# A hand-written order of statements put in another order throughout, the ones written by VectorE, seven warm-up products for six

## The chip, the cores and the metric

The kernel runs on one core of a Trainium2 chip. The metric is the device time of one launch in microseconds (us): the median of 3 runs before was 1338.17 (1337.62 to 1338.43). A core has five engines that each work through a queue of their own, in its order: PE (TensorE, the matrix products, with its weight load PEld), DVE (VectorE), ACT (ScalarE), POOL (GpSimd) and SP (SyncE, which issues most of the transfers here). They are held together by semaphores.

## The reference

A cross-attention in fp32 over 64 batch elements b, with 256 rows of x (512 wide), 256 rows of context (384 wide), and a hidden width of 512:

```
text_p  = einsum('bld,dh->blh', x, W_text) + b_text            # 64 x 256 x 512
audio_p = einsum('bsd,dh->bsh', ctx, W_audio) + b_audio        # 64 x 256 x 512
Q = layer_norm(text_p, g1, beta1)
K = layer_norm(audio_p, g2, beta2)
scores = einsum('blh,bsh->bls', Q, K) / sqrt(512)
alpha  = softmax(scores)
H      = einsum('bls,bsh->blh', alpha, audio_p)
H      = einsum('blh,hk->blk', H, W_out) + b_out
return layer_norm(H + x, g_out, beta_out)
```

## The kernel before

One pass over the 64 batch elements. Everything is placed by hand: the whole body stands under `tc.manual_schedule()`, so each engine gets its instructions in the order in which the statements stand in the file, and the framework adds only the semaphore waits between engines that the tiles need. Each batch element goes through seven stages over several rounds: its x and context are loaded and transposed, q and k are projected and normalised, both go out to DRAM and come back transposed, the scores are made, the softmax, the context z, and the output y with its normalisation. In one round of the steady loop (line 1926, b from 3 to 60, 58 rounds) one element is at the scores (`at`, element b), one at its softmax weights and context (`last`, b-1), one at the end of its context and at the output (`old`, b-2; its output object is `y`), one at the last normalisation (`settled`, b-3), and q and k of element b+2 are projected (`q2`, `k2`), k and q of b+1 turned, x and context of b+3 and b+4 loaded and turned. Ahead of the loop the first rounds are written out statement by statement, and behind it the last ones.

The products are cut so that fewer of them are needed. The scores (`score_part`), the context (`z_part`) and q (`Fork`) use seven half-size products for eight; k and the output use fifteen products of thirds (`Thirds`, 171 wide) in five calls, `one` to `five`. That takes many small sums on the other engines: of halves of q on POOL (`query_step`, L869, tile qsum), of the context on POOL (`c_step`, `e_step`), of z on DVE and POOL (`z_step`, L1084, tile zsum, which reads the PSUM tiles ps_z1 and ps_z2 and the SBUF tile zT), and of results in PSUM on DVE (`dve`, L541).

The steps that the prediction follows, with their lines:

- `y.five()` (L585) is the last group of products of one output; its results stand in ps_m, ps_l, ps_n and ps_u.
- DVE takes them out: `plus_ends` and `plus_middle` (L541, tiles n and u), `plus_n0` (tile d), and `last_11`, `last_10`, `last_01`, `last_00` (L707), which write the finished rows yr with their sums. `last_11` and `last_10` write the same row of yr, and so do `last_01` and `last_00`. Between them stand `add_c22` and `add_c21` (L541, they finish a part of zT from ps_z), `reciprocals` (L956) and `turn_c` (L76, the transposes of the next context).
- ACT writes the rest of zT from PSUM: `copy_top` (L1060, from ps_z1) and `copy_two` (L1114, from ps_z2). Then `copy_n1` (L594), for which DVE's `start_t` waits; the gain and bias of the turned queries, `affine_queries(n)` (L527, tile qT, chunks 0 to 3), and the copy of `after_seven` (L753).
- POOL's `query_step(0)` (L869) makes the first query sum from two chunks, and PE's `score_part(1, 7)` (L884, tile ps_sc) needs it for product 7.
- On SP `load_x_rows` (L97), `store` of q and k (L498), `fetch` of them (L73) and `done.store` (L1369), the finished output, stand in one queue.

At the start `keep_busy(6)` gives PE products of a tile of ones, whose result nobody reads, until the first context is there (L187).

Of the kernel before, what the change touches and what calls it, by code (L numbers as in the profile page):

```python
# [22 lines left out]
def kernel(  # L23
# [87 lines left out]
    nc.gpsimd.memset(ones, 1.0)  # L111
# [1288 lines left out]
    keep_busy(6)  # L1400
# [3 lines left out]
    war = []  # L1404
    pool, tag = (once, 'e')
    war.append(pool.tile([P, HC, P], F32, tag=tag, name=f'war_{0}'))
    arrange(war[0], wa_sb[:, 0, :], HC, nc.gpsimd.tensor_copy)
    mean_wa = means(wa_sb, AC, 'mwa')
    k[0] = Projection('k', 0, c_turn.T, wa_sb, ba_sb, AC, ST, bank[0:2])
    k[0].multiply(0, [0])  # L1410
    k[0].multiply(1, [0])
    k[0].multiply(0, [1])
    x_turn = RowTurn(x_0, DC, 'xT')
    x_turn.tile(0)
    ba_row = ba_sb.rearrange('p (o h) -> p o h', o=1)
    mean_ba = means(ba_row, 1, 'mba')
    k[0].multiply(0, [2])
    x_turn.tile(1)
    pool, tag = (work, 'eT')
    war.append(pool.tile([P, HC, P], F32, tag=tag, name=f'war_{1}'))  # L1420
    arrange(war[1], wa_sb[:, 1, :], HC, nc.gpsimd.tensor_copy)
    pool, tag = (work, 'eT')
    war.append(pool.tile([P, HC, P], F32, tag=tag, name=f'war_{2}'))
    arrange(war[2], wa_sb[:, 2, :], HC, nc.gpsimd.tensor_copy)
    turn_weights(0, 1)
    k[0].multiply(1, [1])
    k[0].multiply(1, [2])
    centre(wa_sb, mean_wa, AC)
    mean_wt = means(wt_sb, DC, 'mwt')
    q[0] = Projection('q', 0, x_turn.T, wt_sb, bt_sb, DC, LT, bank[2:4])  # L1430
    q[0].multiply(0, [0])
    q[0].multiply(0, [1])
    q[0].multiply(1, [0])
    k[0].evict(0)
    wa_t = const.tile([P, 11, WP], F32, tag='wa_thirds', name='wa_thirds')
    third_weights(wa_sb, wa_t, [0])
    k[0].evict(1)
    k[0].scales()
    third_weights(wa_sb, wa_t, [1], nc.vector)
    k[0].normalise([0])  # L1440
    q[0].multiply(1, [1])
    q[0].multiply(0, [2])
    q[0].multiply(0, [3])
    q[0].multiply(1, [2])
    cT[1] = turn_c(1)
    turn_weights(1, 1)
    q[0].multiply(1, [3])
    k[1] = Projection('k', 1, cT.pop(1), wa_sb, ba_sb, AC, ST, bank[4:6])
    k[1].multiply(0, [0])
    bt_row = bt_sb.rearrange('p (o h) -> p o h', o=1)  # L1450
    mean_bt = means(bt_row, 1, 'mbt')
    turn_weights(2, 1)
    centre(wt_sb, mean_wt, DC)
    centre(bt_row, mean_bt, 1)
    wa_blocks = third_weights(wa_sb, wa_t, [3])
    q[0].evict(0)
    k[1].multiply(0, [1])
    k[1].multiply(0, [2])
    bt_step = const.tile([P, H2], F32, tag='bt_step', name='bt_step')
    nc.vector.tensor_tensor(bt_step, bt_sb[:, :H2], bt_sb[:, H2:], ALU.subtract)  # L1460
    k[1].multiply(1, [0])
    q[0].evict(1)
    k[0].normalise([1])
    k[0].store()
    turn_weights(3, 1)
    k[1].multiply(1, [1])
    xT[1] = turn_x(1)
    xs_1 = SumX(xT.pop(1), nc.vector)
    xs_1.add(1)
    wt_blocks = weight_sums(wt_sb, DC // 2, 'wtsum')  # L1470
    load_c(2)
    load_x(2)
    k[1].multiply(1, [2])
    k[0].fetch()
    g1_sb, be1_sb, g2_sb, be2_sb, bac_sb = take_columns()
    fold_multiply(1, 0, 1)
    fold_multiply(1, 1, 2)
    q[0].scales()
    folds.append(p_at.tile([P, H], F32, tag='at', name='ps_fold'))
    fold_multiply(2, 0, 1)  # L1480
    centre(ba_row, mean_ba, 1)
    k[1].evict(0)
    q[0].normalise([0])
    xs_1.add(1)
    k[1].evict(1)
    xs_1.add(1)
    q[0].normalise([1])
    nc.vector.tensor_scalar(g2_sb, g2_sb, scale, None, ALU.mult)
    cT[2] = turn_c(2)
    q[0].store()  # L1490
    fold_multiply(0, 0, 1)
    fold_multiply(0, 1, 2)
    cs[2] = Sides(cT.pop(2), 'csum')
    cs[2].add(1)
    xs[1] = xs_1
    q[1] = Fork(1, xs.pop(1).of, wt_blocks)
    q[1].seven()
    load_c(3)
    cs[2].add(1)
    nc.vector.tensor_scalar(be2_sb, be2_sb, scale, None, ALU.mult)  # L1500
    load_x(3)
    xs_1.add(1)
    cs[2].add(1)
    q[0].fetch()
    Fork.seed()
    q[1].one()
    q[1].after_one()
    fold_multiply(0, 2, 3)
    cs[2].add(1)
    q[1].six()  # L1510
    fold_multiply(2, 1, 2)
    fold_multiply(0, 3, 4)
    q[1].after_seven()
    xT[2] = turn_x(2)
    xs[2] = SumX(xT.pop(2))
    xs[2].add(1)
    part = bias_parts()
    q[1].start_q3()
    k[1].square()
    cs[2].add(1)  # L1520
    fold_evict(0)
    q[1].step_r()
    load_c(4)
    q[1].five()
    at_0 = att[0] = Attention(0)
    at_0.k.turn()
    cs[2].add(1)
    q[1].after_five()
    fold_multiply(1, 2, 3)
    q[1].four()  # L1530
    q[1].two()
    q[1].three()
    k[1].scales()
    third_weights(wa_sb, wa_t, [2], nc.vector)
    k[1].normalise([0])
    k[1].normalise([1])
    k[1].store()
    fold_multiply(1, 3, 4)
    ba_delta = third_bias(ba_sb, 'ba_delta')
    Thirds.seed_with(ba_sb)  # L1540
    load_x(4)
    cs[2].add(1)
    k2_0 = k[2] = Thirds('k', 2, cs.pop(2), wa_blocks, ba_sb, ba_delta)
    k2_0.two()
    q[1].square()
    k2_0.one()
    at_0.affine_keys(0)
    third_weights(wa_sb, wa_t, [4], nc.vector)
    cT[3] = turn_c(3)
    cs[3] = Sides(cT.pop(3), 'csum')  # L1550
    cs[3].add(1)
    q[1].scales()
    k2_0.copy_n1()
    q[1].normalise([0])
    fold_multiply(2, 2, 3)
    Fork.seed()
    xs[2].add(1)
    xs[2].add(1)
    xT[3] = turn_x(3)
    fold_multiply(2, 3, 4)  # L1560
    xs[2].add(1)
    cs[3].add(1)
    k2_0.start_t()
    k2_0.three()
    bias_rest(part, 1, 2)
    q[2] = Fork(2, xs.pop(2).of, wt_blocks)
    q2_0 = q[2]
    q2_0.one()
    at_0.q.turn()
    q[1].normalise([1])  # L1570
    k2_0.copy_t()
    fold_evict(1)
    k2_0.start_l0()
    q[1].store()
    at_0.affine_keys(2)
    at_0.affine_queries(3)
    k2_0.start_l1()
    bias_rest(part, 2, 3)
    cs[3].add(1)
    bias_rest(part, 3, 4)  # L1580
    q2_0.seven()
    fold_evict(2)
    q2_0.after_seven()
    cs[3].add(1)
    q2_0.after_one()
    at_0.affine_keys(1)
    k2_0.four()
    at_0.affine_queries(0)
    q2_0.six()
    k2_0.take_m()  # L1590
    k2_0.start_u()
    cs[3].add(1)
    at_0.affine_queries(1)
    k2_0.five()
    k2_0.copy_u()
    wao_room = const.tile([P, HC * H], F32, tag='wo', name='wao_thirds')
    wao_t = wao_room[:, :11 * WP].rearrange('p (n h) -> p n h', n=11)
    third_weights(wao_sb, wao_t, [1])
    q2_0.start_q3()
    beo_sb = row(beta_out, 'beo')  # L1600
    q2_0.step_r()
    at_0.affine_queries(2)
    k2_0.copy_n()
    q2_0.five()
    q2_0.after_five()
    fold_bias(part)
    cT[4] = turn_c(4)
    k2_0.leave_middle()
    cs[3].add(1)
    at_0.affine_keys(3)  # L1610
    k2_0.leave()
    k2_0.leave_ends()
    xs[3] = SumX(xT.pop(3))
    xs[3].add(1)
    k2_0.middle_d()
    var_0 = small.tile([P, 4], F32, tag='var4', name='var')
    k2_0.square(var_0[:, 2:], [0])
    k2_0.middle_sum()
    xs[3].add(1)
    cs[3].add(1)  # L1620
    k2_0.square(var_0[:, 2:], [1])
    xs[3].add(1)
    q2_0.three()
    q2_0.two()
    k2_1 = k[3] = Thirds('k', 3, cs.pop(3), wa_blocks, ba_sb, ba_delta)
    k2_1.one()
    k2_1.copy_n1()
    xs[3].add(1)
    wao_blocks = third_weights(wao_sb, wao_t, [[0, 3], [4, 2]][0])
    q2_0.square(var_0[:, :2], [0])  # L1630
    q2_0.four()
    k2_0.seed()
    k[1].fetch()
    at_0.score(0, 1)
    at_0.score(1, 2)
    at_0.score(2, 3)
    at_0.score(3, 4)
    at_0.score(4, 5)
    xT[4] = turn_x(4)
    q2_0.square(var_0[:, :2], [1])  # L1640
    at_0.score(5, 6)
    at_0.score(6, 7)
    scales_of(q2_0, k2_0, var_0)
    q2_0.normalise([0])
    q2_0.normalise([1])
    Fork.seed()
    k2_1.start_t()
    k2_1.three()
    at_0.score(7, 8)
    k2_1.two()  # L1650
    k[1].turn([0])
    k2_0.normalise([0])
    cs[4] = Sides(cT.pop(4), 'csum')
    cs[4].add(1)
    k2_0.normalise([1])
    last_1 = att[0]
    last_1.maxima()
    k[1].turn([1])
    q[3] = Fork(3, xs.pop(3).of, wt_blocks)
    q2_1 = q[3]  # L1660
    q2_1.one()
    q2_1.after_one()
    k2_1.copy_t()
    q2_1.seven()
    last_1.exponentials([0])
    q[1].fetch()
    k2_1.start_l1()
    cs[4].add(1)
    q2_1.six()
    last_1.exponentials([1])  # L1670
    k2_1.start_l0()
    last_1.reciprocals()
    k2_1.four()
    q2_1.after_seven()
    q[1].turn()
    k2_1.take_m()
# [249 lines left out]
    for b in range(3, B - 3):  # L1926
# [115 lines left out]
        if done: done.store()  # L2042
# [434 lines left out]
```

## Time and profile before

| | before |
|---|---|
| median of 3 runs | 1338.17 us |
| profiled execution | 1337.96 us |
| its span on the core | 1336.2 us |
| PE busy | 99% |
| DVE busy | 93% |
| ACT busy | 87% |
| POOL busy | 86% |
| share of PE in the chain that ended last | 99% |
| DMA over the span | 240 GB/s |

The span is the time from the first to the last instruction that the profiler saw; the execution is 1.8 us longer. A busy share counts the time in which an engine works, pipelined instructions counted once; a row of a timeline gives the start in us, the duration in us, the engine, the line, the operation and its tiles, and in brackets the idle time ahead of it and what ended it. Starts of neighbouring instructions of one engine can lie closer together than their durations, since they overlap.

### The profile page before, as it was taken

How to read it: one execution, taken by the hardware profiler on the slowest of the kernel's cores; microseconds unless marked ns; L12 is line 12 of the kernel's file. 1: busy time of each engine (PE TensorE's matmuls, PEld its weight loads, DVE VectorE, ACT ScalarE, POOL GpSimd, SP SyncE). 2: the span in 40 equal slices, each digit the busy share in tenths (PEclk: the TensorE clock that was granted, in tenths of full speed). 3: DMA queues.
4: the chain of work that ended last, by engine and by line, in shares of the span. 5: the costliest groups of instructions: out<-in, count | busy, mean ns of one | idle time of the engine just before them, and what ended most of it. 6: DMA issues, size and time to landing. Idle time of an engine off the chain costs nothing.

```text
span 1336.2 us, 29969 instructions
## 1 busy us (share of the span) xinstructions
PE 1329.2 (99%) x8495; PEld 1249.4 (94%) x8495; DVE 1244.4 (93%) x3313; ACT 1163.4 (87%) x3310; POOL 1153.6 (86%) x1855
## 2 busy tenths in 40 slices
PE   9999999999999999999999999999999999999998
PEld 5889999999999999999999999999999999999996
DVE  6669999999999999999999999999999999999968
ACT  4898898898998988888988988989889889889885
POOL 5778898898898988988988988988989889889865
PEclk9999999999999999999999999999999999999999
DMA  9888889989888899888888899889888998888773
GB/s 223 222 243 230 239 252 244 250 244 253 250 246 233 257 250 239 257 246 240 251 245 248 250 244 253 246 232 261 248 234 257 252 240 253 245 243 252 210 233 135
DMA packets 448972, 322.24 MB, mean 241 GB/s; under 512 B 153765, under 2 KB 381349, under 8 KB 448806
## 3 DMA queue, kind: packets, MB, share of 16 engines
q1 hardware_dynamic: 448710, 320.20, 85.8%
q8 instruction: 68, 1.11, 0.4%
q14 instruction: 98, 0.80, 0.2%
q10 hardware_dynamic: 96, 0.13, 0.0%
HBM read 203.57 MB, written 116.65 MB: 240 GB/s over the span
## 4 chain that ended last, share of the span: by engine, by line
PE 99%; ACT 0%; DVE 0%; issue 0%; POOL 0%; ACTq 0%; DVEq 0%; POOLq 0%
PE ps_f L733 29%; PE ps_m L557 16%; PE ps_sc L884 14%; PE ps_n L557 11%; PE ps_u L557 8%; PE ps_z L1033 7%; PE ps_l L557 5%; PE ps_z L1095 5%; PE ps_sc L823 1%; PE ps_f L440 0%; PE ps_m L440 0%; PE ps_n L440 0%; PE ps_l L244 0%; PE ps_u L440 0%; PE ps_fold L244 0%; PE ps_m L244 0%
## 5 line engine op out<-in xcount | busy, mean ns | idle before, releaser
L352 POOL TENSOR_TENSOR csum<-csum,cT 128x256 f32<-128x256 f32 x310 | 195.1, 630 | 5.2
L869 POOL TENSOR_TENSOR qsum<-qT 128x256 f32<-128x256 f32 x118 | 113.0, 958 | 98.7 <-ACT qT L527 92.0
L733 PE MATMUL ps_f<-wtsum,xsum 128*128 128x256 f32 x756 | 194.1, 379 | 0.0
L527 ACT ACTIVATE qT<-qT,columns 128x256 f32<-128x256 f32 x256 | 152.7, 598 | 1.8 <-DVE qT L76 1.8
L733 PEld LDWEIGHTS ps_f<-wtsum,xsum 128*128 128x128 f32 x756 | 131.9, 191 | 11.5 <-issue 0.7
L527 ACT ACTIVATE kT<-kT,columns 128x256 f32<-128x256 f32 x256 | 141.9, 610 | 0.0
L733 PE MATMUL ps_f<-wt,xT 128*128 128x256 f32 x504 | 129.5, 379 | 0.0
L884 PE MATMUL ps_sc<-kT,qT 128*128 128x128 f32 x928 | 122.5, 275 | 0.0
L884 PEld LDWEIGHTS ps_sc<-kT,qT 128*128 128x128 f32 x928 | 114.7, 192 | 0.0
L1357 DVE SCALAR_TENSOR_TENSOR yr<-yr,rstd,beo 128x512 f32<-128x512 f32 x120 | 107.9, 899 | 0.1
L884 PE MATMUL ps_sc<-ksum,qsum 128*128 128x128 f32 x696 | 106.0, 275 | 0.0
L884 PEld LDWEIGHTS ps_sc<-ksum,qsum 128*128 128x128 f32 x696 | 97.8, 191 | 3.4 <-DVE ps_sc L541 0.4
L733 PEld LDWEIGHTS ps_f<-wt,xT 128*128 128x128 f32 x504 | 91.0, 190 | 9.7
L1348 DVE SCALAR_TENSOR_TENSOR yr<-yr,nm,go 128x512 f32<-128x512 f32 x124 | 96.8, 781 | 0.0
L488 ACT ACTIVATE kr<-kr,rstd 128x512 f32<-128x512 f32 x126 | 92.5, 737 | 0.1
L1158 ACT ACTIVATE junk<-yr,nm 128x512 f32<-128x512 f32 x124 | 90.2, 728 | 0.2
L314 POOL TENSOR_TENSOR xsum<-xT 128x256 f32<-128x256 f32 x124 | 90.4, 729 | 0.0
L794 ACT ACTIVATE junk<-ps_f 128x512 f32<-128x512 f32 x126 | 75.3, 598 | 16.8 <-PE ps_f L733 15.4
L541 DVE TENSOR_TENSOR ps_l<-ps_m,t 128x171 f32<-128x171 f32 x248 | 83.6, 337 | 6.2 <-ACT t L605 1.5
L804 ACT ACTIVATE qr<-ps_f,rstd 128x512 f32<-128x512 f32 x126 | 87.9, 700 | 0.1
L520 DVE STREAM_TRANSPOSE kT<-kq 128x512 f32<-128x512 f32 x122 | 85.4, 702 | 1.3 <-DMA kq<-kd 1.2
L1095 PE MATMUL ps_z<-eT,c 128*128 128x256 f32 x296 | 84.4, 380 | 0.0
(302 smaller groups left out, 4657.1 us busy)
## 6 DMA issues: line engine op xcount, KB each, us to landing
kd<-kr SPq DMA_DIRECT2D x64, 512.0 KB, 3.1
kq<-kd SPq DMA_DIRECT2D x256, 128.0 KB, 3.2
qd<-qr SPq DMA_DIRECT2D x64, 512.0 KB, 2.8
qq<-qd SPq DMA_DIRECT2D x256, 128.0 KB, 2.9
xq<-in_x_dram SPq DMA_DIRECT2D x252, 128.0 KB, 3.1
x<-in_x_dram SPq DMA_DIRECT2D x63, 512.0 KB, 5.5
out_dram<-yr SPq DMA_DIRECT2D x62, 512.0 KB, 5.1
cq<-in_ctx_dram SPq DMA_DIRECT2D x252, 96.0 KB, 4.1
```

Source lines behind the costliest of these rows:

```text
L314: self.engine.tensor_tensor(*step)
L352: nc.gpsimd.tensor_tensor(*step)
L488: nc.scalar.mul(row, row, self.r[t])
L527: nc.scalar.activation(self.T[:, k, :], self.T[:, k, :], AF.Identity, bias=bet[:, k : k + 1], scale=gam[:, k : k + 1],)
L557: nc.tensor.matmul(place, lhsT=self.sides.of[n], rhs=self.weights[n], start=(n == 14), stop=True, skip_group_check=True,)
L733: nc.tensor.matmul(place, lhsT=side, rhs=w, start=(n == 7 and c == 0), stop=True, skip_group_check=True,)
L869: nc.gpsimd.tensor_tensor(*self.steps[n])
L884: nc.tensor.matmul(self.place(t, m), lhsT=self.qsides[n][:, c], rhs=self.ksides[n][:, c], start=False, stop=True, skip_group_check=True,)
L1033: nc.tensor.matmul(self.zp[{1: 0, 2: 0, 4: 2}.get(n, 1)], lhsT=self.asides[n], rhs=self.bsides[n], start=(n == 7), stop=True, skip_group_c ...
L1095: nc.tensor.matmul(ps, lhsT=c_rows[self.b][:, s, bass.ts(j, P)], rhs=self.eT[:, s, :], start=start, stop=(s == ST - 1), skip_group_check=True,
L1348: nc.vector.scalar_tensor_tensor(row, row, self.nm[:, t : t + 1], go_sb, ALU.add, ALU.mult)
L1357: nc.vector.scalar_tensor_tensor(self.y[:, t, :], self.y[:, t, :], self.r[t], beo_sb, ALU.mult, ALU.add)
```

## The change

The same statements stand in another order, in the first rounds, in the steady round and at the end. Apart from the order two things differ: the ones are written by VectorE, and `keep_busy` makes seven products of them.

```diff
     ones = once.tile([P, P], F32, tag="u3", name="ones")
-    nc.gpsimd.memset(ones, 1.0)
+    nc.vector.memset(ones, 1.0)
...
-    keep_busy(6)
+    keep_busy(7)
```

The first statements of the steady round, before and now (the lines that say nothing of the steps above are left out):

```diff
     for b in range(3, B - 3):
...
-        old.copy_top()
-        cT[b + 3] = turn_c(b + 3)
-        old.copy_two()
-        q2.seven()
-        at.affine_queries(0)
-        k2.one()
-        k2.copy_n1()
...
-        old.add_c21()
-        old.product_sums()
-        old.z_step(0)
-        at.affine_queries(1)
-        at.query_sums()
-        at.query_step(0)
-        old.z_step(7)
-        q2.after_seven()
-        old.z_step(1)
-        k2.start_t()
...
-        at.score_part(1, 7)
...
+        old.copy_two()
+        k2 = k[b + 2] = Thirds("k", b + 2, cs.pop(b + 2), wa_blocks, ba_sb, ba_delta)
...
+        old.add_c21()
+        last.context_sums()
+        cT[b + 3] = turn_c(b + 3)
+        k2.one()
+        q2 = q[b + 2]
+        q2.seven()
+        old.z_step(0)
+        if done: done.store()
+        at.query_sums()
+        old.copy_top()
+        k2.copy_n1()
+        at.affine_queries(1)
+        at.affine_queries(0)
+        q2.after_seven()
+        k2.start_t()
...
+        at.query_step(0)
...
+        old.z_step(1)
+        at.open_scores()
...
+        at.score_part(1, 7)
```

And its last ones:

```diff
-        y.five()
...
-        at.reciprocals()
-        y.plus_n0()
-        last.add_c22()
-        y.plus_middle(x_old, 0)
-        att[b + 1].affine_keys(3)
-        y.last_10()
...
-        y.last_01(x_old)
-        att[b + 1].key_step(2)
-        y.last_11()
-        at.store_e()
-        k2.fetch()
-        load_x_rows(b - 1)
-        k2.seed()
-        y.last_00()
...
+        k2.normalise([1])
+        load_x_rows(b - 1)
+        k2.normalise([0])
+        k2.store()
...
+        y.five()
+        at.exponentials([0])
+        x_new.add(1)
+        y.plus_ends(x_old)
+        at.exponentials([1])
...
+        y.plus_n0()
+        at.reciprocals()
+        y.last_11()
+        at.divide_e([1])
+        y.last_10()
+        y.plus_middle(x_old, 0)
+        at.divide_e([0])
+        y.last_01(x_old)
+        done = settled
+        at.store_e()
+        y.last_00()
```

What that does to the queues is shown at three places. The first is ACT at the change from one round to the next, from the division of the softmax weights (L960, tile e) to the copy of `after_seven` (L753). L571 and L749 seed PSUM for the next products; qT is the turned query tile. Before:

```order
L960 ACTIVATE e_6608<-e_6608,rden 128x256 [waits Activation_49]
L749 COPY ps_f_90<-ps_f_90 128x256 [waits PE_49]
L571 COPY ps_m<-ba 128x2x171
L1060 COPY zT<-ps_z_6561 128x256 [waits PE_49]
L1114 COPY zT<-ps_z_6671 128x256
L527 ACTIVATE qT_6563<-qT_6563,columns 128x256
L594 COPY n_6691<-ps_n 128x171 [waits DVE_49,PE_49]
L527 ACTIVATE qT_6563<-qT_6563,columns 128x256
L753 COPY s_6705<-ps_f_91 128x256
```

And now, at the same place:

```order
L571 COPY ps_m<-ba 128x2x171 [waits DVE_49]
L749 COPY ps_f_90<-ps_f_90 128x256 [waits PE_49]
L960 ACTIVATE e_6625<-e_6625,rden 128x256 [waits DVE_49]
L960 ACTIVATE e_6625<-e_6625,rden 128x256
L1114 COPY zT<-ps_z_6670 128x256 [waits PE_49]
L1060 COPY zT<-ps_z_6511 128x256 [waits DVE_49,PE_49]
L594 COPY n_6701<-ps_n 128x171 [waits PE_49]
L527 ACTIVATE qT_6567<-qT_6567,columns 128x256 x2
L753 COPY s_6705<-ps_f_91 128x256 [waits PE_49]
```

`copy_top` (L1060) stands behind `copy_two` (L1114) and waits for DVE beside PE; the first of the two query chunks (L527), which stood ahead of `copy_n1` (L594), now stands behind it, next to the second.

The second place is DVE behind `y.five`, from `plus_n0` (d) to the first step of z (L1084); the second row before is `add_c22`, and `plus_ends` stands just ahead of these rows both before and now. Before:

```order
L541 TENSOR_TENSOR d<-ps_n,u 128x171 [waits DVE_49]
L541 TENSOR_TENSOR zT<-ps_z_6561,z_6575 128x128 [waits PE_49]
L541 TENSOR_TENSOR u<-ps_u,x_6386 128x171 [waits DVE_49]
L707 SCALAR_TENSOR_TENSOR yr_6420,totals<-d,ps_n 128x170 [waits DMAHW4_49]
L707 SCALAR_TENSOR_TENSOR yr_6420,totals<-ps_l,x_6386 128x2x171
L707 SCALAR_TENSOR_TENSOR yr_6420,totals<-ps_n,n 128x2x171 [waits DVE_49]
L707 SCALAR_TENSOR_TENSOR yr_6420,totals<-ps_u,u 128x170 [waits DVE_49]
L76 STREAM_TRANSPOSE cT_6683<-cq_6432 128x8x3x32 [waits DMAHW6_49,DMAHW5_49,DMAHW3_49]
L541 TENSOR_TENSOR zT<-ps_z_6561,u_6616 128x128 [waits Activation_49]
L1084 TENSOR_TENSOR zsum<-ps_z_6561,zT 128x256 [waits DVE_49,Activation_49,Pool_49]
```

And now:

```order
L541 TENSOR_TENSOR d<-ps_n,u 128x171 [waits DVE_49]
L956 RECIPROCAL rden<-den 128x2 [waits Activation_49]
L707 SCALAR_TENSOR_TENSOR yr_6399,totals<-ps_n,n 128x2x171 [waits DMAHW3_49]
L707 SCALAR_TENSOR_TENSOR yr_6399,totals<-d,ps_n 128x170 [waits DVE_49]
L541 TENSOR_TENSOR u<-ps_u,x_6333 128x171
L707 SCALAR_TENSOR_TENSOR yr_6399,totals<-ps_l,x_6333 128x2x171
L707 SCALAR_TENSOR_TENSOR yr_6399,totals<-ps_u,u 128x170 [waits DVE_49]
L541 TENSOR_TENSOR zT<-ps_z_6511,u_6617 128x128 [waits PE_49]
L76 STREAM_TRANSPOSE cT_6691<-cq_6490 128x8x3x32 [waits DMAHW6_49,DMAHW7_49,DMAHW5_49,DMAHW4_49]
L1084 TENSOR_TENSOR zsum<-ps_z_6511,zT 128x256 [waits DVE_49,Activation_49,Pool_49]
L541 TENSOR_TENSOR ps_u<-ps_n,n_6701 128x171 [waits Activation_49]
```

The two instructions that write one row (ps_n,n and d,ps_n; ps_l,x and ps_u,u) are now neighbours, each second one with a wait of DVE on itself; `add_c21` (zT from ps_z and u) moved ahead of the transposes, and `start_t` (ps_u from ps_n) ahead of the further steps of z. `add_c21` waited for ACT before and waits for PE now.

The third place is the beginning of DVE's and PE's queues (DVE first, then PE), where a + is a row of now and a - a row of before:

```order
+L111 MEMSET ones 128x128
 L127 MEMSET vectors 128x128
 L179 COPY cTr<-c_107 128x384 x2
 L179 COPY xTr<-x_106 128x512 x2
-L187 MATMUL ps_f_91<-ones 128x128 x6
+L187 MATMUL ps_f_91<-ones 128x128 x7
 L202 MATMUL ps_rows<-ident,cTr 128x128 x6
```

The ones are DVE's first instruction, ahead of the vectors of zeros, and a seventh product stands ahead of the transposes of the first context.

More of the change, by code (lines that the diff above doesn't have):

```diff
@@ L1515 @@
[L1515 removed]
+    nc.vector.tensor_scalar(be2_sb, be2_sb, scale, None, ALU.mult)
+    cs[2].add(1)
+    wa_blocks = third_weights(wa_sb, wa_t, [3])
     xs[2].add(1)
[L1517 to L1520, printed above, removed]
[L1521 to L1532 removed]
```

1500 lines of the change are left out of this document (754 added, 746 removed).

## The prediction

> **What bounds the kernel now.** I read the page first, then the busy times by stretch, the waits, and last the timeline of one steady round, engine by engine. From the page, and from the table of busy times (columns: stretch, its length, then busy time of each engine with its instruction count, granted clock, DMA share, GB/s):
>
> ```profile
> span 1336.2 us, 29969 instructions
> PE 1329.2 (99%) x8495; PEld 1249.4 (94%) x8495; DVE 1244.4 (93%) x3313; ACT 1163.4 (87%) x3310; POOL 1153.6 (86%) x1855
> 0.00:8.00 8.00, 6.43 (x21) 4.67 (x22) 1.27 (x3) 2.86 (x5) 1.98 (x11) 1.00 0.72 212
> 8.00:30.00 22.00, 22.00 (x68) 10.69 (x67) 16.86 (x33) 11.49 (x27) 15.04 (x23) 1.00 0.99 224
> 700.00:720.29 20.29, 20.29 (x136) 19.46 (x135) 19.57 (x54) 18.09 (x53) 18.11 (x30) 1.00 0.87 250
> 1310.00:1337.00 27.00, 21.06 (x93) 15.80 (x91) 20.86 (x50) 13.70 (x36) 13.95 (x17) 0.97 0.26 98
> ```
>
> PE has no idle time in the stretch from 8 to 30 us nor in the round shown, and 1329.2 of 1336.2 in all; a round of the steady loop is 20.29 us of pure matrix work. The change takes no matrix product away, so there is nothing to win in the 58 rounds (the loop runs b from 3 to 60): a new order can only keep PE fed or fail to. What could be won lies in the first 8 us, 8.00 - 6.43 = 1.57, and in the last 27, 27.00 - 21.06 = 5.94, and those are mostly the first load and the last row's normalisation. What could be lost is any wait inside the round, times 58. So the question is one of slack in the round: DVE is busy 19.57 of 20.29, and every chain that leaves PE, crosses other engines and comes back has to fit.
>
> **The start.** The ones now come from DVE.
>
> ```profile
> 1.30 0.20 POOL L111 MEMSET ones<- 128x128 f32 x1
> 1.56 2.93 PE L187 MATMUL ps_f<-ones 128*128 128x128 f32 x12 [1.56 <-POOL ones L111]
> 0.82 0.17 DVE L127 MEMSET vectors<- 128x128 f32 x1 [0.82 <-PEq L2465]
> 3.88 1.20 DVE L179 COPY cTr<-c 128x384 f32<-128x384 f32 x2 [2.90 <-DMA c<-in_ctx_dram]
> 4.49 1.54 PE L202 MATMUL ps_rows<-ident,cTr 128*128 128x128 f32 x6
> ```
>
> DVE's first instruction starts at 0.82, POOL writes the ones at 1.30, so PE can begin 0.48 earlier; the seventh product costs 2.93/6 = 0.49, which takes that up exactly. What follows, the transposes at 4.49, waits for DVE's copy of c at 3.88 and that for a load, which nothing here brings forward. I take 0; the bounds are -0.5 (the whole 0.48 reaches the end) and +0.5 (the seventh product in the way of the transposes). The other statements ahead of the loop and behind it do the same work in another order. Between 8 and 30 us PE had no gap to lose; I take 0, between -1 (some of the last 5.94) and +1.5 (one late input of the size of the 1.57 in the first 8 us).
>
> **The steady round.** One chain changes its form. `y.five` ends with its sums in ps_m, and DVE then runs twelve instructions from `plus_ends` to `add_c21` and `turn_c`, with `z_step(0)` as the thirteenth. Before, ACT's `copy_top` waited for PE alone and had run long before `z_step(0)`; now it waits for DVE too, and the semaphore count that it waits for is the one that `z_step(0)` raises in the built program. Behind `copy_top` in ACT's queue stand `copy_n1`, the affines of query chunks 1 and 0, and `after_seven`. For the affines waits POOL's `query_step(0)`, and for that PE's product 7 of the scores. DVE's side of it, as it ran before (start, duration):
>
> ```profile
> 702.94 0.51 DVE L541 TENSOR_TENSOR n<-ps_m,x 128x342 f32<-128x342 f32 x1
> ...
> 703.99 0.28 DVE L541 TENSOR_TENSOR zT<-ps_z,z 128x128 f32<-128x128 f32 x1
> 704.18 0.33 DVE L541 TENSOR_TENSOR u<-ps_u,x 128x171 f32<-128x171 f32 x1
> 704.42 0.33 DVE L707 SCALAR_TENSOR_TENSOR yr<-d,ps_n 128x170 f32<-128x170 f32 x1
> ...
> 704.67 0.51 DVE L707 SCALAR_TENSOR_TENSOR yr<-ps_l,x 128x342 f32<-128x342 f32 x1
> ...
> 705.79 0.97 DVE L76 STREAM_TRANSPOSE cT<-cq 128x768 f32<-128x768 f32 x1
> 706.69 0.25 DVE L541 TENSOR_TENSOR zT<-ps_z,u 128x128 f32<-128x128 f32 x1
> 707.62 0.41 DVE L1084 TENSOR_TENSOR zsum<-zsum,ps_z 128x256 f32<-128x256 f32 x1
> ```
>
> *DVE.* From 702.94 to 706.69 eleven of the instructions take 3.75; `add_c21` adds 0.19 (704.18 - 703.99, the same operation and size). In the new order `last_11` is followed at once by `last_10`, and `last_01` by `last_00`, each pair writing one row, with a wait of DVE on itself. What such a pair costs stands in the trace ahead of the loop, where they were neighbours already:
>
> ```profile
> 95.32 0.33 DVE L707 SCALAR_TENSOR_TENSOR yr<-d,ps_n 128x170 f32<-128x170 f32 x1
> ...
> 95.68 0.51 DVE L707 SCALAR_TENSOR_TENSOR yr<-ps_n,n 128x342 f32<-128x342 f32 x1
> ...
> 96.12 0.33 DVE L707 SCALAR_TENSOR_TENSOR yr<-ps_u,u 128x170 f32<-128x170 f32 x1
> ...
> 96.50 0.51 DVE L707 SCALAR_TENSOR_TENSOR yr<-ps_l,x 128x342 f32<-128x342 f32 x1
> ```
>
> A 170-wide one is followed after 0.36 and 0.38 here, and after 0.25 in the loop (704.42 to 704.67): 0.11 + 0.13 = 0.24 for the two pairs. `z_step(0)` itself takes 0.41. DVE's part: 3.75 + 0.19 + 0.24 + 0.41 = 4.59 from the start of `plus_ends`.
>
> *ACT and POOL.* Their rows before:
>
> ```profile
> 705.85 0.37 ACT L1060 COPY zT<-ps_z 128x256 f32<-128x256 f32 x1
> 706.12 0.38 ACT L1114 COPY zT<-ps_z 128x256 f32<-128x256 f32 x1
> 707.29 0.30 ACT L594 COPY n<-ps_n 128x171 f32<-128x171 f32 x1 [0.30 <-PE ps_n L557]
> 707.49 0.60 ACT L527 ACTIVATE qT<-qT,columns 128x256 f32<-128x256 f32 x1
> 708.00 0.36 ACT L753 COPY s<-ps_f 128x256 f32<-128x256 f32 x1
> 711.76 0.59 ACT L527 ACTIVATE qT<-qT,columns 128x256 f32<-128x256 f32 x1
> 708.18 0.73 POOL L869 TENSOR_TENSOR qsum<-qT 128x256 f32<-128x256 f32 x1
> 712.43 1.19 POOL L869 TENSOR_TENSOR qsum<-qT 128x256 f32<-128x256 f32 x1 [1.58 <-ACT qT L527]
> ```
>
> `copy_top` holds ACT 0.27 (705.85 to 706.12), `copy_n1` 0.20, the first affine 0.51, the second runs its whole 0.60: 1.58. POOL's step takes 0.73. From engine to engine: ACT to POOL 712.43 - (711.76 + 0.59) = 0.08; POOL to PE 1.56 - (1.30 + 0.20) = 0.06; for DVE to ACT I take 0.05. The chain is 4.59 + 1.58 + 0.73 + 0.19 = 7.09 and ends 702.94 + 7.09 = 710.03 on the clock of this round.
>
> *PE.* Between `y.five` and product 7 stand the same products before and now, in a slightly different order:
>
> ```profile
> 702.74 0.45 PE L557 MATMUL ps_u<-wao_thirds,zT 128*128 128x171 f32 x2
> ...
> 704.55 0.39 PE L1033 MATMUL ps_z<-eT,c 128*128 128x128 f32 x2
> ...
> 709.27 0.50 PE L884 MATMUL ps_sc<-ksum,qsum 128*128 128x128 f32 x3
> 95.22 0.49 PE L1033 MATMUL ps_z<-eT,c 128*128 128x128 f32 x2
> ```
>
> PE would be there at 709.27. Before, `query_step(0)` was done at 708.18 + 0.73 = 708.91, 0.36 ahead of need; now it is 710.03 - 709.27 = 0.76 late. A product that PE had to wait for also starts with nothing loaded behind it: 0.49 after the wait at 95.22 against 0.39 in the stream, 0.10 more. So 0.86 a round, and since the chain starts at PE's own `y.five`, PE's delay moves the next round's chain by as much and nothing makes it up: 58 x 0.86 = 49.9. Bounds: 0.70 a round (engine hops of 0.05, the reload hidden behind another wait's end) gives 40.6; 0.96 (the next products, which need `step_r` from the same ACT queue, pay a second reload) gives 55.7.
>
> [...]
>
> *Transfers.* SP's queue moves too: `load_x_rows` now stands ahead of `k2.store`, so the keys' way out and back starts later by that issue.
>
> ```profile
> 705.75 1.95 SPq L73 DMA_DIRECT2D kq<-kd  x4
> 707.74 0.88 SPq L97 DMA_DIRECT2D x<-in_x_dram  x1
> 712.94 0.70 DVE L520 STREAM_TRANSPOSE kT<-kq 128x512 f32<-128x512 f32 x1
> kq<-kd SPq DMA_DIRECT2D x256, 128.0 KB, 3.2
> ```
>
> The fetch was issued by 705.75 + 1.95 = 707.70 and landed 3.2 later, at 710.9, for a transpose at 712.94: 2.0 of cover against at most 0.88. I take 0; without that cover `turn` and all of DVE behind it would stand 0.88. `done.store` comes earlier in the queue and nobody waits for it in the round.
>
> **Sum.** The profiled execution took 1337.96, span 1336.2 with 1.8 around it; the median of the runs is 1338.17, 0.2 above. 1337.96 + 49.9 + 0 = 1387.9; I say 1388.
>
> **Rivals.** *A: no loss.* DVE is through `z_step(0)` earlier than I add up. If `z_step(0)` is done 0.76 sooner, product 7 is ready when PE comes, PE stays full, and the time is 1337.96 plus or minus the 0.5 of the start, 1337.7 if half of that is won. For it: several waits of DVE for PE and for DMA inside that run are gone or stand elsewhere, and my 0.24 for the pairs and 0.19 for the hops, 0.43 together, may be too much. Against: in the rows above each of DVE's instructions starts before the one ahead has ended, so there was no idle time in the run that could go, and 0.43 is short of 0.76. 8%.
>
> *B: only DVE's own loop is too long.* If the way through PE is covered better than reckoned, DVE still stands between `z_step(0)` and `start_t`: hop 0.05, `copy_top` 0.27, `copy_n1` 0.30, hop 0.08 = 0.70. With the 0.24 of the pairs and its 19.57 of work that is 20.51 against 20.29, 0.22 a round, 12.8 in all: 1351. For it: DVE is the fullest of the four helpers. Against: the way through PE needs 7.09 whatever DVE's sum is. 12%.
>
> *C: POOL's step meets DVE.* `query_step(1)` took 1.19 in this round where `query_step(0)` took 0.73, with DVE's 512-wide instructions running beside it. If the moved step fell beside such a one, 0.46 more a round, 26.7 in all: 1415. [...] Against: behind `z_step(0)` DVE has only short instructions that read PSUM. 8%.
>
> **How the numbers follow.** The forecast has 72%: 1388, alone 1378 to 1396. The range of 8 in 10 reaches down to the upper part of B and up part of the way to C: 1356 to 1400. A measurement of this kernel tells 0.2% (2.7 us) from no change. Faster by over that needs A with a gain at both ends: 4%. Within it, A without: 4%. Slower: all the rest, 92%.
>
> **What would show it.** Right: PE or its weight load waits for POOL's qsum at L869 some 58 times, 0.7 to 0.8 us each; ACT's copy at L1060 waits for DVE's zsum at L1084; a round of 21.1 us, PE busy in some 96% of a steady stretch; DVE, ACT and POOL as busy in total as before. DVE's same-row neighbours at L707 0.11 to 0.13 further apart. The first product near 1.1 us, the transposes of c still near 4.5. Wrong: rounds of 20.3 (A) or 20.5 with PE waiting for DVE and not for qsum (B), or qsum steps of 1.2 in the chain (C). A wait of PE at another product, for a transpose that waits for a load, would say that I followed the wrong chain.

## The result and the profile after

The changed kernel takes 1385.97 us (median of 4 runs, 1384.91 to 1386.67) against 1338.3 before (4 runs): 3.5% slower, ratio 1.0351 with an interval of 1.0333 to 1.0369. The prediction said 1388. The profiled execution took 1385.45, its span 1383.7, so 47.5 more than the span before.

First where the time went. The page of the changed kernel, and the memset of the scores' tile, which runs once a round in both kernels (the view of one line: count, shortest/median/longest in ns, first and last start), of before and then of the change:

```profile
span 1383.7 us, 29786 instructions
PE 1353.1 (98%) x8497; PEld 1250.4 (90%) x8497; DVE 1254.3 (91%) x3314; ACT 1155.3 (83%) x3310; POOL 1167.3 (84%) x1854
```

```profile
L874 DVE MEMSET ps_sc<- x58: 272/272/272, 99.4 to 1256.3; 128x256 f32 x58
```

```profile
L874 DVE MEMSET ps_sc<- x58: 272/272/272, 100.4 to 1304.2; 128x256 f32 x58
```

Between 58 memsets lie 57 rounds: (1256.3 - 99.4) / 57 = 20.30 us before and (1304.2 - 100.4) / 57 = 21.12 now. The 0.82 a round times 58 is 47.7, all of the loss: the start and the end together cost and gain nothing that can be told. PE is counted busy for 1353.1 instead of 1329.2 with one product more. So the busy share hides half of the stall, 23.9 of 47.7: the group of products ahead of the stop is written down as a longer one (ps_u below, 0.53 for 0.45).

The waits of the changed kernel (engine, what waited, for what: total us, times, longest):

```profile
ACT zT L1060 <- DVE zsum L1084: 72.6, 58, 1.4
POOL qsum L869 <- ACT qT L527: 58.4, 58, 1.2
DVE ps_u L541 <- ACT n L594: 45.5, 63, 3.0
PE ps_sc L884 <- DVE ps_sc L874: 22.6, 58, 0.4
```

`copy_top` (L1060) waits for `z_step(0)` (L1084) in each of the 58 rounds, and `start_t` (ps_u, L541) for `copy_n1` behind it. PE, which waited nowhere in the round before, stops 58 times, and the view names the memset of ps_sc, not POOL's qsum. (It also has the weight load of product 1 waiting 35.9 us, 58 times, and names ACT's copy s of L753. That copy cannot be what holds product 1: in a run below, start_t and three later, product 1 starts at 714.13 while the copy runs from 713.80 to 714.16.) The timeline of the round at 711 us, PE first, then DVE, ACT and POOL:

```profile
711.77 0.74 PE L557 MATMUL ps_m<-wa,csum 128*128 128x171 f32 x4
712.45 0.53 PE L557 MATMUL ps_u<-wa_thirds,csum 128*128 128x171 f32 x2
713.37 0.68 PE L884 MATMUL ps_sc<-kT,qT 128*128 128x128 f32 x4 [0.39 <-DVE ps_sc L874]
713.89 0.61 PE L884 MATMUL ps_sc<-ksum,qsum 128*128 128x128 f32 x4
```

```profile
706.76 0.51 DVE L541 TENSOR_TENSOR n<-ps_m,x 128x342 f32<-128x342 f32 x1
...
710.88 0.38 DVE L1084 TENSOR_TENSOR zsum<-ps_z,zT 128x256 f32<-128x256 f32 x1
711.96 0.34 DVE L541 TENSOR_TENSOR ps_u<-ps_n,n 128x171 f32<-128x171 f32 x1 [0.70 <-ACT n L594]
...
712.95 0.27 DVE L874 MEMSET ps_sc<- 128x256 f32 x1
```

```profile
711.35 0.37 ACT L1060 COPY zT<-ps_z 128x256 f32<-128x256 f32 x1 [1.37 <-DVE zsum L1084]
711.62 0.31 ACT L594 COPY n<-ps_n 128x171 f32<-128x171 f32 x1
711.82 1.10 ACT L527 ACTIVATE qT<-qT,columns 128x256 f32<-128x256 f32 x2
```

```profile
713.00 0.73 POOL L869 TENSOR_TENSOR qsum<-qT 128x256 f32<-128x256 f32 x1 [1.00 <-ACT qT L527]
```

The same products of PE in the kernel before (product 7, at 709.27, stands in the prediction):

```profile
707.96 0.74 PE L557 MATMUL ps_m<-wa,csum 128*128 128x171 f32 x4
708.54 0.45 PE L557 MATMUL ps_u<-wa_thirds,csum 128*128 128x171 f32 x2
708.83 0.61 PE L884 MATMUL ps_sc<-kT,qT 128*128 128x128 f32 x4
```

Read from the top: in the round before, ps_u followed ps_m by 0.58 (707.96 to 708.54), product 1 of the scores followed by 0.29 (708.83), and product 7 by 0.44 (709.27). Now the steps are 0.68, 0.92 and 0.52: late by 0.10, 0.63 and 0.08, together 0.81. The first 0.10 belongs to `start_t`: ps_u starts 0.15 behind its end (711.96 + 0.34 = 712.30). Two ways lead from `copy_top` to these products. One is the forecast's: affines, done at 712.92, POOL's qsum, done at 713.73, product 7 at 713.89. The other runs over `copy_n1`, `start_t` at 711.96, two more steps of z and the memset, done at 713.22, to product 1 at 713.37. They end so near each other that this profile cannot say which one costs the time. The experiments were made for that, and for whether `copy_top` is behind both.

### The profile page after: what moved, and what is told of

Same layout as the page of the kernel before. It is cut to its first block, busy times and chain, and to the rows that moved or that the text cites. A ratio compares the mean times of both kernels' runs of the same rounds, so it can differ in the third digit from the quotient of the medians.

```text
span 1383.7 us, 29786 instructions
## 1 busy us (share of the span) xinstructions
PE 1353.1 (98%) x8497; PEld 1250.4 (90%) x8497; DVE 1254.3 (91%) x3314; ACT 1155.3 (83%) x3310; POOL 1167.3 (84%) x1854
## 3 DMA queue, kind: packets, MB, share of 16 engines
q8 instruction: 68, 1.11, 0.4%
## 4 chain that ended last, share of the span: by engine, by line
PE 25%; ACT 24%; DVE 21%; DMA 16%; issue 7%; SPq 6%; DVEq 0%; POOL 0%; ACTq 0%
DMA kd<-kr 8%; PE ps_f L733 6%; SPq L73 6%; PE ps_m L557 4%; ACT kr L488 4%; DVE zsum L1084 4%; ACT kT L527 3%; ACT qr L804 3%; PE ps_sc L884 3%; ACT junk L460 3%; DMA xq<-in_x_dram 3%; DVE yr L1357 2%; ACT junk L794 2%; PE ps_n L557 2%; PE ps_u L557 2%
## 5 line engine op out<-in xcount | busy, mean ns | idle before, releaser
L352 POOL TENSOR_TENSOR csum<-csum,cT 128x256 f32<-128x256 f32 x310 | 250.6, 816 | 0.6
L733 PE MATMUL ps_f<-wtsum,xsum 128*128 128x256 f32 x756 | 184.8, 379 | 0.0
L527 ACT ACTIVATE qT<-qT,columns 128x256 f32<-128x256 f32 x256 | 148.7, 608 | 1.7 <-DVE qT L76 1.7
L884 PE MATMUL ps_sc<-kT,qT 128*128 128x128 f32 x928 | 127.0, 280 | 22.7 <-DVE ps_sc L874 22.6
L733 PEld LDWEIGHTS ps_f<-wtsum,xsum 128*128 128x128 f32 x756 | 136.1, 190 | 14.0 <-issue 0.5
L884 PEld LDWEIGHTS ps_sc<-kT,qT 128*128 128x128 f32 x928 | 112.6, 191 | 36.5 <-ACT s L753 35.9
L527 ACT ACTIVATE kT<-kT,columns 128x256 f32<-128x256 f32 x256 | 142.9, 619 | 1.4 <-DVE kT L520 1.4
L869 POOL TENSOR_TENSOR qsum<-qT 128x256 f32<-128x256 f32 x118 | 86.3, 732 | 59.2 <-ACT qT L527 58.4
L1357 DVE SCALAR_TENSOR_TENSOR yr<-yr,rstd,beo 128x512 f32<-128x512 f32 x120 | 125.4, 1045 | 0.0
L1023 POOL TENSOR_TENSOR esum<-eT 128x256 f32<-128x256 f32 x59 | 43.2, 732 | 89.5 <-DVE eT L76 85.8
L541 DVE TENSOR_TENSOR ps_l<-ps_m,t 128x171 f32<-128x171 f32 x248 | 82.0, 331 | 5.3 <-ACT t L605 3.0
L488 ACT ACTIVATE kr<-kr,rstd 128x512 f32<-128x512 f32 x126 | 85.1, 732 | 0.1
L541 DVE TENSOR_TENSOR ps_u<-ps_n,n 128x171 f32<-128x171 f32 x124 | 42.2, 341 | 45.5 <-ACT n L594 45.5
```

Of the source, the lines that this page charges most:

```text
L352: nc.gpsimd.tensor_tensor(*step)
L488: nc.scalar.mul(row, row, self.r[t])
L527: nc.scalar.activation(self.T[:, k, :], self.T[:, k, :], AF.Identity, bias=bet[:, k : k + 1], scale=gam[:, k : k + 1],)
L541: nc.vector.tensor_tensor(o, i0, i1, op)
L733: nc.tensor.matmul(place, lhsT=side, rhs=w, start=(n == 7 and c == 0), stop=True, skip_group_check=True,)
L884: nc.tensor.matmul(self.place(t, m), lhsT=self.qsides[n][:, c], rhs=self.ksides[n][:, c], start=False, stop=True, skip_group_check=True,)
```

## The experiments

Each is an edit of the changed kernel, but for the third, which edits the kernel before. Times are medians; the ratio is to the runs of the kernel before in the same set, whose median was 1339.95 in the first four, 1340.3 in the next four and 1339.82 in the last two. The round comes from the row of the memset, as above.

| | time, us | ratio and interval | round, us |
|---|---|---|---|
| old round put back | 1340.09 | 1.0002 (0.9993 to 1.0011) | 20.33 |
| copy_top ahead of z_step(0) | 1340.94 | 1.0008 (0.9999 to 1.0017) | 20.33 |
| before, with copy_top behind z_step(0) | 1414.26 | 1.0549 (1.0531 to 1.0568) | 21.60 |
| same-row pairs apart | 1379.93 | 1.0294 (1.0279 to 1.0310) | 21.00 |
| affines first | 1386.54 | 1.0347 (1.0331 to 1.0362) | 21.12 |
| whole queue first | 1357.5 | 1.0131 (1.0116 to 1.0146) | 20.62 |
| start_t and three later | 1385.75 | 1.0339 (1.0314 to 1.0363) | 21.11 |
| both ways shortened | 1368.3 | 1.0208 (1.0188 to 1.0229) | 20.82 |

**The old round put back.** The steady loop of the kernel before, between the new first statements and the new end.

> The changed kernel with the old steady round put back: the new first statements, the new end, VectorE's ones and seven products stay. Theory (all of the loss lies in the 58 rounds): 1338, within 1.5 us of the kernel before. Rival (part of the loss is made at the start and the end, or the round takes over a backlog from the new start): over 1343.

1340.09, no difference to the kernel before that can be told. So the loss is in the loop, and the new start (VectorE's ones, seven products) and the new end are worth nothing either way.

**copy_top ahead of z_step(0).** One statement of the loop is moved:

```diff
         old.add_c21()
+        old.copy_top()
         last.context_sums()
...
         old.z_step(0)
-        old.copy_top()
         k2.copy_n1()
```

> The changed kernel with one statement moved: copy_top stands right behind add_c21, ahead of turn_c and z_step(0), all else as in the change. Theory (copy_top behind z_step(0) holds ACT, and with it start_t, the memset of the scores, the affines and query_step(0)): copy_top starts 1.2 us earlier in the round, by more than the 0.82 that a round lost, so PE waits no more and the time is 1338 to 1342. Rival (the loss is spread over the new order: POOL's longer sums, the same-row pairs on DVE, more transfers at one time): under half comes back, over 1362.

1340.94: of the 46 that lay between the two kernels 45 are back. The stretch of one round, and ACT's row in it:

```profile
700.00:720.33 20.33, 20.33 (x136) 19.50 (x135) 19.94 (x54) 18.08 (x53) 18.32 (x30) 1.00 0.83 240
```

```profile
707.85 0.39 ACT L1114 COPY zT<-ps_z 128x256 f32<-128x256 f32 x1
708.23 0.37 ACT L1060 COPY zT<-ps_z 128x256 f32<-128x256 f32 x1
```

`copy_top` follows `copy_two` after 0.38, where it followed after 1.73 in the changed kernel (709.62 to 711.35), and PE is busy in all of the 20.33. The place of this one statement is the whole loss; 179 others stand where the change put them.

**before, with copy_top behind z_step(0).** The same defect put into the kernel before, with the change's order on ACT:

```diff
-        old.copy_top()
...
-        at.affine_queries(0)
         k2.one()
-        k2.copy_n1()
...
         old.z_step(0)
+        old.copy_top()
+        k2.copy_n1()
         at.affine_queries(1)
+        at.affine_queries(0)
```

> The kernel before with copy_top, copy_n1 and both affines put behind z_step(0), in the change's order on ACT; all else as before. Theory: copy_top starts at z_step(0)'s end + 0.09, then 0.27 + 0.20 + 1.10 on ACT, 0.08, 0.73 on POOL, 0.06 to 0.16: product 7 of the scores comes 0.73 to 0.82 late, 1380 to 1386. Rival (the order on ACT alone does little, and it takes the rest of the new order too): under 1355.

1414.26: the loss is there, and 28 us above the theory's range. PE's first stop is the theory's: product 7 stands 2.06 behind ps_m (704.76 to 706.82) where 1.31 would do (707.96 to 709.27), 0.75 late for the 0.73 to 0.82 that were said. The waits, and PE's second stop, which the theory did not have:

```profile
ACT zT L1060 <- DVE zsum L1084: 82.3, 58, 1.7
ACT ps_m L571 <- DVE kr L541: 32.6, 58, 1.1
DVE zsum L1084 <- ACT zT L1060: 28.9, 58, 0.8
```

```profile
713.23 0.82 PE L557 MATMUL ps_n<-wao,zsum 128*128 128x171 f32 x4 [0.17 <-DVE kr L541]
```

In this order DVE waits for `copy_top` in its turn (28.9 over 58 rounds, 0.50 each) and so comes late to the sums of k (kr). For them waits ACT's next seed of ps_m, 0.56 a round, and PE stops once more, at the first products of y. Those start 1.19 behind the group before them (712.04), which had followed its own by 0.87 (711.17). The mechanism is confirmed. Its price in another order was not to be had by carrying the chain of one round over.

**Same-row pairs apart.**

```diff
         y.last_11()
-        at.divide_e([1])
-        y.last_10()
         y.plus_middle(x_old, 0)
-        at.divide_e([0])
         y.last_01(x_old)
+        y.last_10()
+        at.divide_e([1])
+        at.divide_e([0])
```

> The changed kernel with VectorE's last sums in the order last_11, plus_middle(0), last_01, last_10, last_00, so that no two neighbours write one row. Theory (these two waits of DVE on itself lie on the chain, 0.22 to 0.24 a round): 13 us come back, 1371 to 1375. Rival (they do not lie on the path that sets the end, or the waits only move): 1385 to 1387.

1379.93: 6 of the 13 us come back, which neither had. DVE's four sums in the changed kernel, then its rows here, and PE's last product of z here:

```profile
707.94 0.49 DVE L707 SCALAR_TENSOR_TENSOR yr<-ps_n,n 128x342 f32<-128x342 f32 x1
...
708.47 0.33 DVE L707 SCALAR_TENSOR_TENSOR yr<-d,ps_n 128x170 f32<-128x170 f32 x1
...
708.98 0.50 DVE L707 SCALAR_TENSOR_TENSOR yr<-ps_l,x 128x342 f32<-128x342 f32 x1
...
709.52 0.34 DVE L707 SCALAR_TENSOR_TENSOR yr<-ps_u,u 128x170 f32<-128x170 f32 x1
```

```profile
706.05 0.49 DVE L707 SCALAR_TENSOR_TENSOR yr<-ps_n,n 128x342 f32<-128x342 f32 x1
...
706.47 0.33 DVE L541 TENSOR_TENSOR u<-ps_u,x 128x171 f32<-128x171 f32 x1
706.72 0.51 DVE L707 SCALAR_TENSOR_TENSOR yr<-ps_l,x 128x342 f32<-128x342 f32 x1
...
707.14 0.33 DVE L707 SCALAR_TENSOR_TENSOR yr<-d,ps_n 128x170 f32<-128x170 f32 x1
...
707.40 0.33 DVE L707 SCALAR_TENSOR_TENSOR yr<-ps_u,u 128x170 f32<-128x170 f32 x1
...
707.77 0.29 DVE L541 TENSOR_TENSOR zT<-ps_z,u 128x128 f32<-128x128 f32 x1
```

```profile
707.35 0.39 PE L1033 MATMUL ps_z<-eT,c 128*128 128x128 f32 x2
```

Each 342-wide sum is followed after 0.42 now, where a same-row neighbour followed after 0.53 and 0.54. The pairs did cost 0.23. But `add_c21` needs PE's last product of z, which ends at 707.35 + 0.39 = 707.74, and starts at 707.77, 0.37 behind its neighbour instead of 0.26. From `plus_ends` to `add_c21` the run is 2.91 (704.86 to 707.77) against 3.02 (706.76 to 709.78): 0.11 is left, 58 times of which is 6.4.

**Affines first, and start_t later.** These two take one of the two ways away each. Affines first:

```diff
         old.copy_two()
+        at.affine_queries(1)
+        at.affine_queries(0)
...
         old.copy_top()
         k2.copy_n1()
-        at.affine_queries(1)
-        at.affine_queries(0)
```

> The changed kernel with affine_queries(1) and (0) put right behind copy_two on ACT, into the 1.37 that ACT stands idle ahead of copy_top. Theory (two ways in one: copy_n1, start_t, the steps of z and the memset still wait for copy_top, so product 1 stays where it was): only the 0.08 at product 7 comes back, 1379 to 1384. Rival (the chain of the prediction alone, affines to query_step(0) to product 7): all comes back, 1338 to 1345.

1386.54, nothing came back, not even the 0.08 at product 7. POOL, DVE and PE:

```profile
712.49 0.73 POOL L869 TENSOR_TENSOR qsum<-qT 128x256 f32<-128x256 f32 x1
```

```profile
713.49 0.27 DVE L874 MEMSET ps_sc<- 128x256 f32 x1
```

```profile
713.91 0.68 PE L884 MATMUL ps_sc<-kT,qT 128*128 128x128 f32 x4 [0.39 <-ACT t L605]
714.43 0.61 PE L884 MATMUL ps_sc<-ksum,qsum 128*128 128x128 f32 x4
```

qsum is done at 713.22, long before product 7 at 714.43, and product 7 still follows product 1 by 0.52. So in the changed kernel the 0.08 there was no wait for qsum either, it goes with the stop at product 1. Product 1 starts 0.15 behind the end of the memset (713.76). The bracket names ACT's t (713.56 to 713.86), which product 1 does not read; the memset ends last among what it needs, and product 1 stands 0.15 behind it as in the changed kernel. The way over `start_t` and the memset holds PE by itself for all of the 0.82.

The other way was tried first in a form that is no fair test:

> The changed kernel with start_t behind z_step(1) on VectorE, as it was before the change. In the changed kernel PE stops at product 1 of the scores, released by the memset of ps_sc, and product 7 stands close behind the qsum that it needs. With start_t moved the two steps of z and the memset come 0.46 earlier, so the memset's release of product 1 goes from 713.37 to some 712.99. Theory (two ways in one: product 7's sum on POOL is done at 713.73 whatever the memset does): nothing comes back, 1383 to 1387. Rival (the memset alone sets the stop, product 7 only follows): 0.38 a round come back, 1362 to 1367.

> Both edits at once: start_t behind z_step(1), both affines behind copy_two. Theory (each way alone holds PE, together they are open): the products of k2.two for start_t are now last, 0.35 a round late, 1357 to 1363. Rival (another wait of about the same length stands behind): over 1375.

Both put `start_t` behind `k2.three` too. There it overwrites product 9 of k's projection, which is left out of the result, and it has to wait for that product first: 1404.18 and 1404.13 us, ratio 1.0476 (1.0459 to 1.0494) and 1.0479 (1.0463 to 1.0495), with DVE waiting 28.8 us at `start_t` in the first. (The view names ACT's qT there, which `start_t` does not read; in the round at 722 us product 9 ends at 723.10 and `start_t` starts at 723.21.) They say nothing on the question. With `three` moved along:

```diff
         k2.copy_n1()
...
-        k2.start_t()
...
-        k2.three()
         old.z_step(1)
+        k2.start_t()
+        k2.three()
         at.open_scores()
```

> The changed kernel with start_t behind z_step(1) on VectorE, and k2.three behind start_t, so that product 9 is added to what start_t wrote, as in the changed kernel. The memset of ps_sc comes some 0.46 earlier, product 1 could start at 713.07 on the profiled round's clock (the first affine's end 712.92 + 0.15) where it started at 713.37. Theory (a second way of the same length: the qsum of product 7 is done at 713.73, and a product starts 0.15 after its release, at 713.88 as now): 1383 to 1387. Rival (the way over start_t and the memset is the only one that holds PE, as it holds it alone with the affines moved): 0.3 a round come back, 1366 to 1371.

1385.75, again nothing. The memset, POOL's sum and PE:

```profile
713.62 0.27 DVE L874 MEMSET ps_sc<- 128x256 f32 x1
```

```profile
713.98 0.73 POOL L869 TENSOR_TENSOR qsum<-qT 128x256 f32<-128x256 f32 x1 [1.01 <-ACT qT L527]
```

```profile
713.77 0.53 PE L557 MATMUL ps_u<-wa_thirds,csum 128*128 128x171 f32 x2 [0.27 <-DVE ps_u L541]
714.13 0.61 PE L884 MATMUL ps_sc<-kT,qT 128*128 128x128 f32 x4
714.77 0.71 PE L884 MATMUL ps_sc<-ksum,qsum 128*128 128x128 f32 x4
```

Product 1 now follows ps_u without a wait for the memset, which was done 0.24 before, and product 7 stands 0.64 behind product 1 and 0.06 behind the end of qsum (714.71). Here the forecast's chain is seen with its own stop, and the round is as long as in the changed kernel (21.11 against 21.12). One thing keeps this from being as clean a test as the run before: `start_t` now stands behind `z_step(7)`, which waits 0.49 for `copy_top`, and holds ps_u by 0.43 (712.76 to 713.77, where 0.58 would do), so PE is late by that way too. That qsum alone would cost the whole is read from its row and not from the time: its chain does not run over `start_t`, so product 7 could not start before 714.71 whatever ps_u does.

**Both ways shortened.** Both edits at once.

> The same with both affines right behind copy_two, so that both ways are shorter. Theory: start_t is what is late now, k2.two's last product 0.35 a round, and up to 0.08 for the stopped stream: 1358 to 1366. Rival (a third wait of the old length stands behind the two): over 1375.

1368.3, some 18 back; the theory's range was missed by 2.3. PE's only stop is now at ps_u, for `start_t` (the bracket names POOL's qsum, done at 704.26, which ps_u does not read):

```profile
703.88 0.34 DVE L541 TENSOR_TENSOR ps_u<-ps_n,n 128x171 f32<-128x171 f32 x1
```

```profile
703.35 0.74 PE L557 MATMUL ps_m<-wa,csum 128*128 128x171 f32 x4
704.36 0.53 PE L557 MATMUL ps_u<-wa_thirds,csum 128*128 128x171 f32 x2 [0.27 <-POOL qsum L869]
704.73 0.61 PE L884 MATMUL ps_sc<-kT,qT 128*128 128x128 f32 x4
```

`start_t` ends at 704.22 and ps_u starts 0.14 later, 1.01 behind ps_m where 0.58 would do, and product 1 follows after 0.37 for 0.29: 0.43 + 0.08 = 0.51 a round, where 0.35 was expected for the first part. That there were two ways is shown: neither edit alone gave anything, together they gave 0.30 a round. The 0.51 that is left still comes from `copy_top`: `z_step(7)` waits 0.49 a round for it (28.6 us in all), and `start_t` stands behind that step.

**Whole queue first.** `copy_top` stays behind `z_step(0)`, and what stood behind it goes ahead of it.

```diff
         old.copy_two()
+        at.affine_queries(1)
+        at.affine_queries(0)
...
         old.z_step(0)
...
+        k2.copy_n1()
         old.copy_top()
-        k2.copy_n1()
-        at.affine_queries(1)
-        at.affine_queries(0)
```

> The changed kernel with both affines behind copy_two and copy_n1 ahead of copy_top: copy_top still waits for z_step(0), but only the copy of after_seven stands behind it. Theory (the cost lies in what is queued behind copy_top; of that only z_step(7), z_step(1) and the memset are left, which need copy_top's own result, 0.2 a round): 1349 to 1354. Rival (copy_top's own lateness is the cost, whatever stands behind it): over 1375.

1357.5, some 28 back, 3.5 us above the expected range. DVE and PE:

```profile
718.31 0.34 DVE L541 TENSOR_TENSOR ps_u<-ps_n,n 128x171 f32<-128x171 f32 x1
...
719.44 0.27 DVE L874 MEMSET ps_sc<- 128x256 f32 x1
```

```profile
719.34 0.45 PE L557 MATMUL ps_u<-wa_thirds,csum 128*128 128x171 f32 x2
719.86 0.68 PE L884 MATMUL ps_sc<-kT,qT 128*128 128x128 f32 x4
720.38 0.61 PE L884 MATMUL ps_sc<-ksum,qsum 128*128 128x128 f32 x4
```

`start_t` comes in time. The memset still needs two steps of z that read what `copy_top` wrote or come behind it; it ends at 719.71, product 1 starts 0.15 later and 0.23 late, and product 7 another 0.08 late. So 0.50 of the 0.82 a round was the queue behind `copy_top`, and the rest is its own result that the steps of z wait for.

## Why the prediction was right

**What bounds the kernel, and where a loss could be.** Right: PE still sets the time, the loss is 58 times one stall, and with the old round put back nothing is left of it.

**The start: 0.** Right. VectorE's ones let PE begin at 1.04 where it began at 1.56, the products of ones take 3.35 for 2.93 with the seventh, which takes up 0.42 of that 0.52, and the transposes of c start at 4.66 for 4.49, behind DVE's copy of c at 3.96 for 3.88; nothing of that can be told in the time.

**The chain through DVE, ACT and POOL.** Right in each of its members, to a few hundredths. From `plus_ends` to the end of `z_step(0)` it said 4.59, and it was 711.26 - 706.76 = 4.50; the 0.41 that it took for `z_step(0)` was read from the row of the next step (zsum<-zsum,ps_z is `z_step(1)`), and `z_step(0)` itself took 0.38. `copy_top` 0.27, `copy_n1` 0.20, both affines 1.10 for 1.11, the hop to POOL 0.08 and qsum 0.73 are as said. The hop from DVE to ACT was 0.09 for 0.05. The chain ended 713.73 + 0.06 - 706.76 = 7.03 behind `plus_ends`, with the 0.06 from POOL to PE that the run of start_t and three later shows; 7.09 was said. Product 7 came at 7.13, since product 1 ahead of it was late. The 0.24 for the same-row pairs was 0.23, but only 0.11 of it could be had back, because PE's last product of z stands close behind.

**What PE loses: 0.86 a round.** The size was 0.82; 58 x 0.04 = 2.3 is about the whole distance of 2.0 from 1388 to the result. In the sum stood 0.76 for the chain and 0.10 for a stream that starts with nothing loaded: in the kernel before, the weight load of the product at 95.22 starts at 95.21, after a wait of 0.43, and in the stream that of the product at 704.55 starts at 704.34. In the changed kernel these parts cannot be seen, since product 7 did not wait there. Where it did wait, in the run of start_t and three later, product 7 came 0.70 late (712.76 to 714.77, 2.01 for 1.31), and the group behind it followed after 0.55 (at 715.32) for 0.45: the 0.10 is there.

**Where PE stops.** Here the mechanism had a hole, in one step: "For the affines waits POOL's `query_step(0)`, and for that PE's product 7 of the scores" follows one of two ways only. PE's waits name the memset at product 1, and the sign that was given, 58 waits for qsum, did not show in the changed kernel. It showed as soon as the memset was earlier: with start_t and three later, PE's weight load waits 58 times for qsum, 12.7 us in all. The second way, from `copy_n1` over `start_t` and the steps of z to the memset, had been looked at as far as `start_t`: the idle time of 0.70 reckoned there in rival B is the 0.70 in the row of `start_t`. It was weighed as a matter of DVE's sum and not as a chain that comes back to PE. Both ways are equally long to within 0.1 us, and so the time came out right from the one that does not hold PE in the changed kernel. That is luck: had the second way been half a microsecond longer, 1388 would have been too low by some 29 us. Of the other signs, a share of 96% for PE in a steady stretch came out as 98% (20.73 of 21.12), for half of the stall is counted as busy.

**The rivals.** A (no loss) fell: ACT waits 58 times, 72.6 us in all, for `z_step(0)`. B (only DVE's own loop, 1351) fell: DVE has 1.4 of 21.12 to spare in the round (19.75 busy), and PE is what stops. Half of B's sign did show, since PE waits for DVE and not for qsum, but in rounds of 21.12 and not of 20.5. C (a slow sum on POOL) fell: the view of the line gives qsum a median of 731 ns and a longest of 751, against 738 and 1265 before. What made the long ones before, no run here shows.

Whether `copy_top` must wait for another reader of ps_z1 is not shown: no run left the wait out. What the trace shows is the wait itself: ACT stood 1.25 a round (72.6 / 58) behind a DVE step that writes nothing of what `copy_top` reads. The two steps share ps_z1, which both read, and the tile zT, which `copy_top` writes and `z_step(0)` reads in another part. The waits in DVE's queue speak against zT as the cause: `add_c21` writes zT too, and before, where it followed `copy_top`, a reader of ps_z1, it waited for ACT; now, where it follows only `copy_two`, which writes zT and reads ps_z2, it does not. The order of the two readers is what can be chosen, and that was worth 45 us.

**Transfers.** The earlier `load_x_rows` cost nothing, as said: DVE's waits for the keys (kT for kq) are 2.2 us in three places of the whole span, against 1.2 in one before, and none of them comes back each round.

## What to carry to other kernels

Here ACT's copy from a PSUM tile waited 1.25 us a round for a DVE sum that only reads that tile and stands ahead of it in the program, and with the copy listed first it followed its neighbour after 0.38 without a wait. So try the reader with the longer queue behind it first: one copy behind a sum of 0.38 cost 3.5% here. When a wait in an in-order queue comes late, follow everything that stands behind it in that queue, and everything that waits for that, back to the bound engine; two ways of equal length hid each other here, and a fix of one alone showed nothing (1386.54 and 1385.75 for 1385.97, both together 1368.3). A releaser that a view names can be a bystander: here s, t and qT of ACT were named where the reads of the waiting instruction, or the times, rule them out. In a kernel that runs at 99% of one engine, read a regression from the starts of consecutive instructions, not from busy shares: 3.5% more time showed here as 98% for 99% of PE.

## What was not expected of the hardware

A stop of PE cost more than the wait. A product started 0.14 to 0.15 behind the end of the DVE instruction that released it (713.22 to 713.37, 719.71 to 719.86, 704.22 to 704.36), and the group behind a stopped one came another 0.08 to 0.10 late (0.52 for 0.44, 0.37 for 0.29, 0.55 for 0.45) though its row names no wait. Behind the end of POOL's qsum the first product stood only 0.06 (714.71 to 714.77), and at the start of the changed kernel 0.05 behind the end of DVE's ones (0.82 + 0.17 = 0.99 to 1.04); what makes the difference no run here shows.

Of the 47.7 us that PE lost, 22.6 stand in the view as waits; most of the rest is counted as busy time, 1353.1 for 1329.2: groups of products overlap in the records, and the one whose successor was late is counted in full. The ps_u group counted 0.29 before product 1 covered it, and counts 0.53 ahead of the stop; with the 0.39 of the view that is the 0.63.
